# A second Strassen step shared by pairs of text units, in the output projection of a two-attention block

## The chip, the cores and the metric

One core of one Trainium2 chip. The metric is device time in microseconds (us) of one execution of the whole program; lower is better. TensorE is PE in the profile, its weight loads PEld, VectorE is DVE, ScalarE is ACT, GpSimd is POOL, and SyncE is SP.

## What is computed

The input x is 2 batches of 2048 rows of 640 float32, beside a context of 2 x 128 rows of 384, whose last 4 rows are "adapter" tokens. There are 8 heads of 80 columns.

```
query = x @ Wq;  keyt = ctx[:, :124] @ Wk;  valt = ctx[:, :124] @ Wv
hs = mha(query, keyt, valt)                    # text attention, 2048 x 124 scores a head
ca_q1 = einsum(adapter, Wq_ca)[:, indices, :]
ca_hs1 = mha(ca_q1, x, x)                      # adapter attention, x is key and value
ca_hs2 = mha(ca_hs1 @ Wq, adapter @ Wk_ca, adapter @ Wv_ca)
out = (hs + ca_hs2) @ Wout + b_out + x
```

Everything is float32. The place of the change is the product hs @ Wout for the text path.

## The kernel before, in words

**Units.** The 4096 rows of x are 16 *text units* m of 256 rows, each two tiles i of 128 rows. For a unit the kernel computes scores (`sc`), a softmax (`p`, `r`), turns the probabilities with DVE (`eb`), stores them to DRAM (`kept<-eb`) and takes them back turned as `pT`. Then `text_out_fast(m)` does three products `ph` (hidden rows, turned: features on the partitions), copies them on ACT or DVE into a set of buffers `hs` and a fifth chunk of 128 features that lies in a buffer named `wout_sums`, and makes four sums s1 to s4 of blocks of `hs` on DVE or POOL.

**The first Strassen step.** hs of a unit is split in 2 halves of its rows by 2 halves of its first 512 features, Wout in 2 by 2 with halves of 320 columns (`HALF`). With sums t1 to t4 of the weight blocks (`wsum`, in `wout_sums`, too) seven instead of eight block products give the output, and the last 128 features are multiplied plainly (the "fifth"). The products are put into four *chains* `po_m_0` to `po_m_3` of 4, 2, 1 and 1 steps. A chain keeps one PSUM bank of 128 x 320: a step's matmuls add to what is there, then DVE adds the bank into a half row tile of x (tiles `x_more` or `last_rows`), and the next step of the chain waits for that add, since it changes the bank. So the place of the output that a step belongs to gets all that the chain has summed so far. There are 8 such adds in a unit and 128 in all.

**by_columns.** Every block product runs as four matmuls of 128 x 32 weights, on four strips of columns side by side, 4 to a chunk of 128 features. In the order, "32x320 x8" is a product of two chunks. In the trace a float32 matmul has two records, so that product has 16.

**Order.** Nothing is scheduled at run time. `Desk` issues the operations of all coroutines in the order of a table `TURNS` written into the kernel, from the path of a coroutine to a number for each of its operations: the smallest number goes next, and its remainder by 6 names the engine. Each engine then runs its own instructions in that order, waiting on semaphores where its operands are not there. A step, its add and the next step are operations of one coroutine, so the table has to place them one after another, but other work of PE and of DVE stands between them.

**Other rooms.** `kept` stores, one for each half unit, are 32 in all; the exponentials of the adapter path use buffers `e`, `eb`, `rests`, `landing` and `q` that are free once text scores, softmax and stores are done. Rows of x, 8 tiles, are held from their load until the unit's store. For the last unit (15) the output is stored in halves of a row as each is ready; for others POOL first adds the adapter's rows by an indirect DMA (`add_second`).

Helpers collect line numbers. Before, L396 is any matmul, L405 the matmuls of `by_columns`, L427 an operation of DVE, ACT or POOL, L447 a DMA. After, they are L424, L433, L455 and L475.

Of the kernel before, what the change touches and what calls it, by code (L numbers as in the profile page):

```python
# [14 lines left out]
P = 128  # L15
# [50 lines left out]
class Desk:  # L66
# [393 lines left out]
def kernel(  # L460
# [410 lines left out]
    def one(op):  # L871
        yield op
# [199 lines left out]

    def wq_turned():

        yield Do("DVE", lambda: columns(wq_sb, wq4), [("wq", c) for c in range(5)], marks=["wq4"])
        for i in range(NCH):
            if i < 4:
                op = yield Do("NONE", lambda at: wide_rows[at[0]], [], needs=[(first_rows, 1)])
# [1513 lines left out]
```

## Time and profile before

| what | value |
|---|---|
| median of 3 executions | 573.56 us (573.53 to 573.89) |
| the profiled execution | 572.92 us, of which its span 570.9 us |
| PE busy | 563.0 us, 99%, 8069 records |
| PEld busy | 309.6 us, 54% |
| DVE busy | 394.5 us, 69%, 659 records |
| ACT busy | 287.1 us, 50% |
| POOL busy | 160.1 us, 28% |
| matmuls `po` by columns | 2304 records of 128 x 320 |
| granted PE clock | 1.0 |

The span is what the profile's records cover; the time of the profiled execution is 2.02 us above it. Busy shares are means over the span: the first 400 us hold the adapter path, text scores and softmax, the last 160 us mainly `ph`, the output products and the rest of the adapter path.

### The profile page before, as it was taken

The page shows a single profiled execution, that of the slowest core. Times are in us where ns is not written, and L with a number is a line of the kernel's source. Part 1 is how long each engine was busy: PE and PEld are TensorE (multiplying, and loading weights), DVE is VectorE, ACT ScalarE, POOL GpSimd, SP SyncE. Part 2 cuts the span into 40 slices and gives each one's busy share as a digit, 9 for nine tenths or more (in the row PEclk, how much of TensorE's full clock was granted, in tenths as well). Part 3 has the DMA queues.
Part 4 walks back from the last instruction along what each step waited for, and adds up shares of the span by engine and source line. Part 5 has one row for each costly group of instructions (what it writes and reads, how often), then busy time and mean ns, then how long its engine had stood idle before and what let it go on. Part 6 is the DMA issues. An engine that isn't in the chain of part 4 may idle for free.

```text
span 570.9 us, 18875 instructions
## 1 busy us (share of the span) xinstructions
PE 563.0 (99%) x8069; PEld 309.6 (54%) x8069; DVE 394.5 (69%) x659; ACT 287.1 (50%) x806; POOL 160.1 (28%) x213
## 2 busy tenths in 40 slices
PE   8999999999999999999999999999999999999997
PEld 8885335455555455466554554555555554455553
DVE  4366999999998577458999999998332213544443
ACT  2021355645566899899885754534554664100000
POOL 9102041114440731100004350531203053045152
PEclk9999999999999999999999999999999999999999
DMA  8998476965968977446646979987476587788888
GB/s 245 219 239 141 125 160 154 175 179 133 209 214 153 221 177 214 149 123 201 228 153 201 328 187 316 224 241 228 94 248 131 167 185 243 251 217 212 255 182 209
DMA packets 145691, 113.21 MB, mean 198 GB/s; under 512 B 82548, under 2 KB 116980, under 8 KB 145608
## 3 DMA queue, kind: packets, MB, share of 16 engines
q1 hardware_dynamic: 137144, 95.43, 59.9%
q0 software_dynamic: 5632, 10.69, 11.6%
q10 hardware_dynamic: 2832, 5.90, 3.0%
q8 instruction: 63, 1.03, 0.8%
q14 instruction: 20, 0.16, 0.1%
HBM read 71.60 MB, written 40.39 MB: 196 GB/s over the span
## 4 chain that ended last, share of the span: by engine, by line
PE 93%; ACT 3%; DVE 3%; DMA 1%; issue 0%; SPq 0%; ACTq 0%
PE po L405 28%; PE pq L405 24%; PE sc L396 8%; PE acc L396 7%; PE ph L396 7%; PE s L396 7%; PE pq L396 4%; PE pyz L396 2%; ACT ea L427 2%; PE pv L396 1%; DVE mx L427 1%; PE pk L396 1%; DMA xz<-in_x_dram 1%; ACT p L427 1%; PE pt_wq L410 1%; PE pw L396 0%
## 5 line engine op out<-in xcount | busy, mean ns | idle before, releaser
L427 ACT ACTIVATE p<-sc,m 128x124 f32<-128x124 f32 x256 | 90.4, 382 | 43.0 <-DVE m L427 38.0
L427 DVE TENSOR_REDUCE mx<-s 128x4 f32<-128x2048 f32 x48 | 109.0, 2270 | 1.9 <-PE s L396 1.9
L427 ACT ACTIVATE ea<-s 128x2048 f32<-128x2048 f32 x48 | 90.5, 1886 | 30.9 <-PE s L396 30.5
L405 PE MATMUL po<-wout_sums,hs 128*32 128x320 f32 x1024 | 78.4, 434 | 0.1
L405 PE MATMUL po<-wout_sb,hs 128*32 128x320 f32 x928 | 72.3, 433 | 0.0
L427 POOL TENSOR_TENSOR p<-p,r 128x992 f32<-128x992 f32 x17 | 31.4, 1849 | 130.9 <-DVE r L427 130.9
L405 PE MATMUL pq<-xt,wq_sb 128*32 128x256 f32 (+1 forms) x928 | 66.4, 418 | 0.0
L427 DVE TENSOR_TENSOR last_rows<-last_rows,po 128x320 f32<-128x320 f32 x60 | 28.0, 480 | 44.0 <-PE po L405 43.8
L427 ACT ACTIVATION_READ_ACCUMULATOR p<-sc,m 128x1 f32 x256 | 57.2, 223 | 0.0
L427 DVE TENSOR_TENSOR x_more<-x_more,po 128x320 f32<-128x320 f32 x68 | 32.3, 480 | 34.2 <-PE po L405 33.7
L405 PEld LDWEIGHTS po<-wout_sums,hs 128*32 128x32 f32 x1024 | 33.4, 110 | 32.7 <-issue 2.7
L427 DVE TENSOR_REDUCE m<-sc 128x4 f32<-128x496 f32 x64 | 40.7, 661 | 14.1 <-PE sc L396 14.0
L396 PE MATMUL acc<-ea,y_sb 128*32 128x384 f32 (+2 forms) x768 | 50.2, 382 | 0.2 <-ACT ea L427 0.2
L396 PE MATMUL ph<-pT,vpad 128*32 128x256 f32 x768 | 47.7, 381 | 0.0
L405 PEld LDWEIGHTS po<-wout_sb,hs 128*32 128x32 f32 x928 | 30.1, 110 | 28.3 <-issue 1.6
L2351 POOL DMA_INDIRECT x_more<-o,query x17 | 26.6, 1564 | 65.2 <-DVE x_more L427 31.1
L405 PEld LDWEIGHTS pq<-xt,wq_sb 128*32 128x32 f32 x928 | 27.7, 110 | 28.0 <-issue 13.5
L427 ACT COPY hs<-ph 128x512 f32<-128x512 f32 (+1 forms) x25 | 13.4, 552 | 57.7 <-PE ph L396 57.7
L427 DVE STREAM_TRANSPOSE eb<-p 128x1024 f32<-128x1024 f32 x32 | 39.4, 1232 | 1.2 <-POOL p L427 1.1
L396 PEld LDWEIGHTS sc<-kmain,q 64*128 64x128 f32 x512 | 31.8, 187 | 12.6 <-issue 5.8
L427 POOL TENSOR_TENSOR hs<-hs 128x256 f32<-128x256 f32 x31 | 28.9, 1020 | 33.7 <-ACT hs L427 25.4
L396 PE MATMUL sc<-kmain,q 64*128 64x124 f32 x512 | 38.0, 285 | 0.0
(219 smaller groups left out, 834.4 us busy)
## 6 DMA issues: line engine op xcount, KB each, us to landing
kept<-eb SPq DMA_DIRECT2D x32, 512.0 KB, 3.5
pT<-kept SPq DMA_DIRECT2D x16, 1024.0 KB, 8.0
landing<-away SPq DMA_DIRECT2D x15, 512.0 KB, 4.8
xi<-in_x_dram SPq DMA_DIRECT2D x56, 128.0 KB, 4.2
x_more<-in_x_dram SPq DMA_DIRECT2D x17, 320.0 KB, 5.0
last_rows<-in_x_dram SPq DMA_DIRECT2D x15, 320.0 KB, 4.8
y<-yt SPq DMA_DIRECT2D x16, 256.0 KB, 3.9
y_sb<-y SPq DMA_DIRECT2D x32, 128.0 KB, 4.0
```

The source lines that it names most:

```text
L396: self.pin(self.nc.tensor.matmul(out, lhsT, rhs, **kw))
L405: self.pin(self.nc.tensor.matmul(out[j : j + 32], lhsT[:, j : j + 32], rhs, **kw))
L410: self.pin(self.nc.tensor.transpose(out, in_, ident))
L427: self.pin(getattr(engine, what)(*args, **kw))
L2351: desk.pin(nc.gpsimd.indirect_dma_start(out=t, out_offset=None, in_=o2_of[b], in_offset=bass.IndirectOffsetOnAxis(ap=query[:, st : st + 1] ...
```

## The change

**Pairs.** Ten of the sixteen units form five pairs, (6,7), (3,12), (9,14), (10,11) and (8,15), and units take their turns with the output in the order 0, 4, 2, 1, 5, 13, then the pairs, instead of 0 to 15. A paired unit keeps chain 0 (4 steps) and the product s3·t3, whose bank is now added to two places of the output. The other three block products of the first step, a01·w10, s4·w11 and a11·t4, are taken out of the unit. For each of them the two units of a pair are laid one above the other, 256 rows by 256 features by 320 columns, and that is split again in 2 by 2 by 2: `joint` makes seven products of 128 rows, 128 features and 160 columns instead of eight, in four chains `pi_n_p_c` of 4, 2, 1 and 1 steps (n the pair, p = 0, 1, 2 the block product, c the chain), with the fifth chunk's products in the last steps of the chains. Each of their 8 steps is followed by a DVE add of 128 x 160 into a quarter of a row tile: 24 for a pair.

**Inner sums.** `take_inner` waits for all `kept` stores, then takes the freed buffers (`e`, named `p_0` and `p_1` in the order, `eb`, `rests`, `landing`, one `q`) and makes 12 inner sums of the weights, `inner_w`, once. `joint` makes 8 sums of hs blocks for a pair, `inner_x` (4 of 256 columns, 4 of 128), on DVE or POOL.

**Last unit and beginning.** The last unit's one single-step chain left, s3·t3, is computed in two column halves of 160, and its first tile is stored in quarters of a row. In `wq_turned` the copy `wq4` is forked off, and the first transposes of a chunk wait for that chunk of Wq alone.

**TURNS** is replaced as a whole; a line of it:

```diff
-        ".1": [1025], ".2": [44, 59, 60, 84, 96, 108, 114, 120, 126, 132, 150, 174, 198, 210, 234, 1002], ".3":
```

The core of the rest:

```diff
-        yield Do("DVE", lambda: columns(wq_sb, wq4), [("wq", c) for c in range(5)], marks=["wq4"])
+        yield Fork(one(Do("DVE", lambda: columns(wq_sb, wq4), [("wq", c) for c in range(5)], marks=["wq4"])), 2)
...
-                op = yield Do("PE", turn, ["wq4"], needs=[(banks, 1)])
+                op = yield Do("PE", turn, ["wq4" if c0 else ("wq", i)], needs=[(banks, 1)])
...
+        if m in pair_of_unit:
+            chains = (chains[0], (((s3, t3, None), [("hs", m, "s3")], ((1, 1), (1, 0))),))
...
+    PAIRED = ((6, 7), (3, 12), (9, 14), (10, 11), (8, 15))
...
+    def take_inner():
+        yield Do("NONE", lambda: None, ["wsum"] + [("kept", m, k) for m in range(UNITS) for k in range(2)])
+        op = yield Do("NONE", lambda *z: None, [], needs=[(es, 2), (ebs, 1), (rests, 2), (landing, 1), (qslots, 1)])
...
+    def joint(n, pair):
...
+            steps_of = (
+                (([(a[0][0], w[0][0])], [], (0, 0)), ([(s2, t2)], x(1), (1, 0)), ([(s1, t1)], x(0), (0, 1)),
+                 ([fifth(1, 1)], ends_h, (1, 1))),
+                (([(s3, t3)], x(2), (1, 1)), ([(a[1][1], t4), fifth(1, 0)], ends_h, (1, 0))),
+                (([(a[0][1], w[1][0]), fifth(0, 0)], ends_h, (0, 0)),),
+                (([(s4, w[1][1]), fifth(0, 1)], x(3) + ends_h, (0, 1)),),
+            )
+            for c, steps in enumerate(steps_of):
+                yield Fork(inner_chain(n, pair, p, c, steps, (of4 if p == 1 else []) + ends_h + rows_in, rank), rank)
...
+    def inner_chain(n, pair, p, c, steps, ready, rank):
...
+            op = yield Do(
+                "PE", product, after + at + ready, needs=[(banks, 1)] if k == 0 else [], mode=(P, 32), rank=rank
+            )
...
+            def add(r=r, v=v, po=po):
+                t = xr_of[pair[r]][i][0][:, u * HALF + v * HALF // 2 : u * HALF + (v + 1) * HALF // 2]
+                desk.b_tensor_tensor(t, t, po[:, : HALF // 2], ALU.add)
+            op = yield Do(
+                "DVE", add, [op.at], frees=[(banks, s)] if end else [], marks=[("isum", n, p, r, v, c)], rank=1
+            )
+            at = [op.at]
```

**What it moves.** In the whole program the matmul instructions of the output products by columns go from 1152 of 320 columns to 784 of 320 and 676 of 160. PSUM adds on DVE go from 128 of 128x320 to 106, with 124 of 128x160 beside them.

On PE at the very end, where unit 15's chains close, before (`po_15_0` is the chain of four steps; the number behind a name is its buffer's):

```order
L405 MATMUL po_15_0_7039<-wout_sums_4129,hs_0_4130 32x320 x8
L405 MATMUL po_15_3_7094<-wout_sb_100,hs_0_4130 32x320 x12
L405 MATMUL po_15_1_7110<-wout_sums_4129,hs_0_4130 32x320 x8
L405 MATMUL po_15_0_7039<-wout_sums_4129,hs_0_4130 32x320 x8
L405 MATMUL po_15_1_7110<-wout_sums_4129,hs_0_4130 32x320 x8
L405 MATMUL po_15_1_7110<-wout_sb_100,hs_0_4130 32x320 x4
L405 MATMUL po_15_0_7039<-wout_sb_100,hs_0_4130 32x320 x4
```

The same place after (`pi_4_...` are the products of the fifth pair, units 8 and 15; rows with `wout_sums` on the right of the comma are the fifth chunk):

```order
L433 MATMUL po_15_0_None_7573<-wout_sb_100,hs_1_4231 32x320 x8
L433 MATMUL pi_4_1_0_7453<-wout_sb_100,wout_sums_4140 32x160 x4
L433 MATMUL po_15_1_0_7591<-wout_sums_4140,hs_1_4231 32x160 x8
L433 MATMUL po_15_0_None_7573<-wout_sums_4140,hs_1_4231 32x320 x8
L433 MATMUL pi_4_0_0_7431<-wout_sb_100,wout_sums_4140 32x160 x4
L433 MATMUL pi_4_1_1_7562<-p_1_844,hs_1_4231 32x160 x4
L433 MATMUL pi_4_1_1_7562<-wout_sb_100,wout_sums_4140 32x160 x4
L433 MATMUL po_15_0_None_7573<-wout_sums_4140,hs_1_4231 32x320 x8
L433 MATMUL pi_4_2_1_7425<-inner_w_5507,hs_1_4231 32x160 x4
L433 MATMUL pi_4_2_1_7425<-wout_sb_100,wout_sums_4140 32x160 x4
L433 MATMUL po_15_0_None_7573<-wout_sb_100,wout_sums_4140 32x320 x4
L433 MATMUL po_15_1_1_7654<-wout_sums_4140,hs_1_4231 32x160 x8
```

Between two steps of `po_15_0` there were three products of 320 or one; now there are pieces of 160, and before its last step two pieces of four matmuls. The first half of s3·t3 has moved ahead, the second closes the program.

On DVE, where the inner sums of the weights are made, before (`last_rows` and `x_more` are row tiles, `eb` turned probabilities):

```order
L427 TENSOR_TENSOR p_0_830<-p_0_830,r_1_15_5049 128x32x31
L427 STREAM_TRANSPOSE eb_15_1_5489<-p_0_830 128x1024
L427 TENSOR_TENSOR hs_0_4130<-hs_0_4130 128x256
L427 TENSOR_TENSOR last_rows_4240<-last_rows_4240,po_6_2_5452 128x320
L427 COPY hs_2_5064<-ph_7_2_5514 128x512
```

And after; the last `eb` row is now that of unit 12:

```order
L455 STREAM_TRANSPOSE eb_12_1_5429<-p_1_844 128x1024
L455 COPY wout_sums_4140<-ph_6_4_5431 128x256
L455 COPY hs_2_5067<-ph_7_0_5453 128x512
L455 TENSOR_TENSOR x_more_3084<-x_more_3084,po_5_1_None_5465 128x320
L455 TENSOR_TENSOR last_rows_4230<-last_rows_4230,po_13_1_None_5311 128x320
L455 TENSOR_TENSOR inner_w_5507<-wout_sums_4140 128x160 x2
L455 COPY hs_2_5067<-ph_7_2_5477 128x512
L455 TENSOR_TENSOR p_0_843<-wout_sb_100 128x160
L455 TENSOR_TENSOR p_1_844<-wout_sb_100,p_1_844 128x160
```

Four rows stand between the last turn of probabilities and the first write into the buffer `inner_w`, which is the room of an `eb` before it.

More of the change, by code (lines that the diff above doesn't have):

```diff
@@ L2247, in probabilities @@
         op = yield Do(
-            "NONE", lambda z: wide("pT", z[0], f"pT_{m}"), needs=[(pTs, 1)], marks=[("back", m)],
+            "NONE", lambda z: wide("pT", z[0], f"pT_{m}"), needs=[(pTs, 1)], marks=[("back", m), ("taken", m)],
         )
@@ L2457, in product @@
                         by_columns(
-                            to[:, :HALF], l, r, start=(k == 0 and c == 0), stop=(c == len(pairs) - 1),
+                            to[:, cols], l, r[:, cols], start=(k == 0 and c == 0), stop=(c == len(pairs) - 1),
                             skip_group_check=True,
@@ L2489, in text_out_fast @@
             if m < UNITS - 1:
-                yield Fork(stored(m, i, reads[i, 0] + reads[i, 1]), 1)
+                yield Fork(stored(m, i, reads[i, 0, 0] + reads[i, 1, 0]), 1)
             else:
                 for u in range(2):
-                    yield Fork(stored_half(m, i, u, reads[i, u]), 1)
+                    for v in range(2) if i == 0 else (None,):
+                        yield Fork(stored_half(m, i, u, v, reads[i, u, 0] + reads[i, u, 1] if v is None else reads[i, u, v]), 1)
         for n, steps in enumerate(chains):
-            yield Fork(chain(n, steps), 30 + m)
+            for part in (0, 1) if n in apart else (None,):
+                yield Fork(chain(n, steps, part), 30 + turn_of[m])
@@ L2497, with inner_of_w @@
     fast_of = {}
-    def stored_half(m, i, u, ends):
+    PAIRED = ((6, 7), (3, 12), (9, 14), (10, 11), (8, 15))
+    pair_of_unit = {m: (n, r) for n, pair in enumerate(PAIRED) for r, m in enumerate(pair)}
+    inner_w, inner_x, xjs = [], [], Room(0)
+    OF_HS = {0: (0, 0), 1: (0, 1), 2: (1, 0)}
+    def inner_of_w(p):
+        if p == 2:
+            w = wsum[3]
+        else:
+            w = wout_sb[:, 2:4, p * HALF : (p + 1) * HALF]
+        return [[w[:, k, n * HALF // 2 : (n + 1) * HALF // 2] for n in range(2)] for k in range(2)]
@@ new lines, in take_inner, with less @@
+    def take_inner():
+        yield Do("NONE", lambda: None, ["wsum"] + [("kept", m, k) for m in range(UNITS) for k in range(2)])
+        op = yield Do("NONE", lambda *z: None, [], needs=[(es, 2), (ebs, 1), (rests, 2), (landing, 1), (qslots, 1)])
+        at_q = op.slots[4][0]
+        t = late["pool"].tile([P, 4 * HEADS * R], F32, tag="eb", name="inner_w")
+        flat = [e.rearrange("p h n -> p (h n)") for e in late["e"]] + [t]
+        inner_w.extend(t[:, : 2 * HALF].rearrange("p (s n) -> p s n", s=4) for t in flat)
+        for p in range(3):
+            w, to = inner_of_w(p), inner_w[p]
+            for i, x, y, after in (
+                (0, w[0][1], w[0][0], []), (2, w[1][1], w[0][1], []), (1, w[1][1], to[:, 0], [("iw", p, 0)]),
+                (3, w[1][0], to[:, 1], [("iw", p, 1)]),
+            ):
+                def less(to=to, i=i, x=x, y=y):
+                    (desk.g_tensor_tensor if desk.engine == "POOL" else desk.v_tensor_tensor)(to[:, i], x, y, ALU.subtract)
+                yield Fork(one(Do(("DVE", "POOL"), less, after, rank=0, marks=[("iw", p, i)])), 0)
+        yield Do("NONE", lambda: None, [("iw", p, i) for p in range(3) for i in range(4)], marks=["inner w"])
+        t = q_slot(at_q, "inner_x0")
+        a = late["pool"].tile([P, 2 * 4 * P], F32, tag="rests", name="inner_x1")
+        b = late["pool"].tile([P, 4, 2 * P], F32, tag="landing", name="inner_x2")
+        for ends, middle in ((t.rearrange("p s n -> p (s n)")[:, : 8 * P], t[:, 2:3].rearrange("p s n -> p (s n)")),
+                             (a, b.rearrange("p s n -> p (s n)")[:, : 4 * P])):
+            inner_x.append((
+                ends.rearrange("p (s q n) -> p s q n", s=4, q=2), middle.rearrange("p (s n) -> p s n", s=4),
+            ))
+            xjs.at.append(desk.now)
@@ new lines, in joint, with sums, fifth @@
+    def joint(n, pair):
+        rank = 30 + turn_of[pair[0]]
+        of2 = [("hsT", m, 2) for m in pair]
+        of4 = [("hs", m, "s4") for m in pair]
+        op = yield Do("NONE", lambda z: z[0], of2 + ["inner w"], needs=[(xjs, 1)])
+        at_x = op.value
+        ends, middle = inner_x[at_x]
+        hs = [fast_of[m][0][0] for m in pair]
+        last = [[fast_of[m][0][1][:, i * P : (i + 1) * P] for i in range(2)] for m in pair]
+        five = [wout_sb[:, 4, u * HALF : (u + 1) * HALF] for u in range(2)]
+        outer = [[hs[r][:, 2 + k].rearrange("p (q t) -> p q t", q=2) for k in range(2)] for r in range(2)]
+        inner = [[hs[r][:, 7].rearrange("p (c t) -> p c t", c=2)[:, k] for k in range(2)] for r in range(2)]
+        for name, a, to, after in (("e", outer, ends, of2), ("m", inner, middle, of4)):
+            for i, x, y, op_of, more in (
+                (2, a[0][0], a[1][0], ALU.subtract, []), (0, a[1][0], a[1][1], ALU.add, []),
+                (1, to[:, 0], a[0][0], ALU.subtract, [("ix", n, name, 0)]),
+                (3, a[0][1], to[:, 1], ALU.subtract, [("ix", n, name, 1)]),
+            ):
+                def sums(to=to, i=i, x=x, y=y, op_of=op_of):
+                    (desk.g_tensor_tensor if desk.engine == "POOL" else desk.v_tensor_tensor)(to[:, i], x, y, op_of)
+                yield Fork(one(Do(("DVE", "POOL"), sums, after + more, marks=[("ix", n, name, i)], rank=1)), 1)
+        ends_h = [("hsT", m, 4) for m in pair]
+        rows_in = [("xr", m) for m in pair]
+        for p in range(3):
+            name, a, s = ("m", inner, middle) if p == 1 else (
+                "e", [[outer[r][k][:, p // 2] for k in range(2)] for r in range(2)], ends[:, :, p // 2]
+            )
+            w, t = inner_of_w(p), inner_w[p]
+            i_, u_ = OF_HS[p]
+            def fifth(r, v, i_=i_, u_=u_):
+                return last[r][i_], five[u_][:, v * HALF // 2 : (v + 1) * HALF // 2]
+            s1, s2, s3, s4 = [s[:, i] for i in range(4)]
+            t1, t2, t3, t4 = [t[:, i] for i in range(4)]
+            x = lambda i, name=name: [("ix", n, name, i)]
+            steps_of = (
[7 more added lines that the diff above has]
+                yield Fork(inner_chain(n, pair, p, c, steps, (of4 if p == 1 else []) + ends_h + rows_in, rank), rank)
+        yield Do(
+            "NONE", lambda: None, [("inner", n, p, c) for p in range(3) for c in range(4)], frees=[(xjs, at_x)],
+            marks=[("joined", n)],
+        )
@@ new lines, in inner_chain, with product @@
+    def inner_chain(n, pair, p, c, steps, ready, rank):
+        po, s, at = None, None, []
+        for k, (pairs, after, (r, v)) in enumerate(steps):
+            def product(s=None, k=k, pairs=pairs):
+                to = bank(s[0], f"pi_{n}_{p}_{c}") if s else po
+                for j, (l, w) in enumerate(pairs):
+                    by_columns(
+                        to[:, : HALF // 2], l, w, start=(k == 0 and j == 0), stop=(j == len(pairs) - 1),
+                        skip_group_check=True,
+                    )
+                return to
+            op = yield Do(
+                "PE", product, after + at + ready, needs=[(banks, 1)] if k == 0 else [], mode=(P, 32), rank=rank
+            )
+            if k == 0:
+                po, s = op.value, op.slots[0][0]
+            end = k == len(steps) - 1
+            if end:
+                desk.event(("inner", n, p, c)).t = op.at.t
+            i, u = OF_HS[p]
+            def add(r=r, v=v, po=po):
+                t = xr_of[pair[r]][i][0][:, u * HALF + v * HALF // 2 : u * HALF + (v + 1) * HALF // 2]
+                desk.b_tensor_tensor(t, t, po[:, : HALF // 2], ALU.add)
+            op = yield Do(
+                "DVE", add, [op.at], frees=[(banks, s)] if end else [], marks=[("isum", n, p, r, v, c)], rank=1
+            )
+            at = [op.at]
@@ L2501, in stored_half, with inner_sums @@
+    def inner_sums(m, i, u):
+        n, r = pair_of_unit[m]
+        for p in range(3):
+            if OF_HS[p] == (i, u):
+                at = {(0, 0): (0, 2), (1, 0): (0, 1), (0, 1): (0, 3), (1, 1): (0, 1)}
+                return [("isum", n, p, r, v, c) for v in range(2) for c in at[r, v]]
+        return []
+    def stored_half(m, i, u, v, ends):
         b, st = tiles(m)[i]
         cols = slice(u * HALF, (u + 1) * HALF)
+        if v is not None:
+            cols = slice((2 * u + v) * HALF // 2, (2 * u + v + 1) * HALF // 2)
@@ L2505, in stored_half @@
         to = out[b, st * P : (st + 1) * P, cols]
[L2506 removed]
+        yield Do(("SP", "ACT"), lambda: dma(to, t[:, cols], 0.43 if v is None else 0.25, 0.45, 2.2))
     def stored(m, k, both):
```

60 lines of the change are left out of this document (38 added, 22 removed), and 439 rows, old and new, of the table TURNS.

## The prediction

> **What bounds the kernel now.** I read the page first: busy time, the slices, the chain that ended last.
>
> ```profile
> span 570.9 us, 18875 instructions
> PE 563.0 (99%) x8069; PEld 309.6 (54%) x8069; DVE 394.5 (69%) x659; ACT 287.1 (50%) x806; POOL 160.1 (28%) x213
> PE   8999999999999999999999999999999999999997
> DVE  4366999999998577458999999998332213544443
> PEclk9999999999999999999999999999999999999999
> PE 93%; ACT 3%; DVE 3%; DMA 1%; issue 0%; SPq 0%; ACTq 0%
> ```
>
> PE is busy in every slice at full granted clock, and 93% of the chain is PE. So matmul time taken away shortens the kernel, unless PE has to wait. DVE is full in slices 5 to 12 and 19 to 28 and then drops to 2 to 5 tenths. Then the windows of the last 160 us, where the products of the change lie (start and end, length, busy time and count of PE, PEld, DVE, ACT, POOL, clock, DMA):
>
> ```profile
> 400.00:440.00 40.00, 40.00 (x652) 20.36 (x648) 14.03 (x27) 21.93 (x15) 9.48 (x7) 1.00 0.59 155
> 440.00:480.00 40.00, 40.00 (x646) 20.00 (x639) 10.21 (x22) 23.64 (x18) 9.23 (x10) 1.00 0.76 212
> 480.00:520.00 40.00, 40.00 (x623) 20.01 (x619) 18.54 (x46) 6.31 (x10) 13.60 (x11) 1.00 0.82 217
> 520.00:560.00 40.00, 40.00 (x620) 22.32 (x612) 17.88 (x42) 1.54 (x3) 18.62 (x14) 1.00 0.84 206
> ```
>
> PE never waits here, and DVE has 60.7 us of work in 160 (14.03 + 10.21 + 18.54 + 17.88). Last, PE's list of waits: for whom, how long in all, how often, the longest.
>
> ```profile
> PE s L396 <- DVE mx L427: 1.1, 2, 0.7
> PE pt_x L410 <- DVE first_rows L427: 0.4, 1, 0.4
> ```
>
> There is little to win from waits, so the sum is about streamed columns, and about the waits that the change can bring.
>
> **The stream.** The products by columns, and stretches of the timeline of PE in which such matmuls run without a stop (start, length, count):
>
> ```profile
> L405 PE MATMUL po<-wout_sums,hs 128*32 128x320 f32 x1024 | 78.4, 434 | 0.1
> L405 PE MATMUL po<-wout_sb,hs 128*32 128x320 f32 x928 | 72.3, 433 | 0.0
> L405 PE MATMUL po<-wout_sb,wout_sums 128*32 128x320 f32 x352 | 31.1, 432 | 0.0
> ...
> 388.00 2.34 PE L405 MATMUL po<-wout_sb,hs 128*32 128x320 f32 x32
> 390.16 1.26 PE L405 MATMUL po<-wout_sums,hs 128*32 128x320 f32 x16
> 391.35 0.44 PE L410 MATMUL pm<-ident,mt 128*128 128x128 f32 x2
> ...
> 52.89 1.00 PE L396 MATMUL pvca<-w_vca,caT 128*32 128x160 f32 x24
> 53.70 1.90 PE L405 MATMUL pq<-xt,wq_sb 128*32 128x512 f32 x16
> ```
>
> The 2304 records are the 1152 matmuls. Four run side by side, so one's 433 ns isn't its price: that is the distance of the starts, (390.16 - 388.00)/32 = 67.5 ns a record. The trace has records of 160 columns in the same shape of tile, too: (53.70 - 52.89)/24 = 33.75 ns, half. The change takes away 368 matmuls of 320, 736 records, 49.7 us, and adds 676 of 160, 1352 records, 45.6 us. That is **-4.05 us**. The starts are rounded to 0.01 us, which is 0.6 us over the 1352 records and 0.2 over the others.
>
> What speaks against so clean a half are the weight loads, one to each record whatever its width:
>
> ```profile
> 52.89 0.67 PEld L396 LDWEIGHTS pvca<-w_vca,caT 128*32 128x32 f32 x20 [0.30 <-issue]
> ```
>
> Twenty take 0.67 us, 33.5 ns each, just under the 33.75 of the matmuls beside them. They are hidden with nothing to spare. On this the Trainium skill, "TensorE: Matmul & The Clock Gate", section "Back-to-back issue gap", says that in a stream of load and matmul pairs both set the spacing, about 81 ns at 128 columns where the formula for one alone gives 56. If 160-column records paid that ratio, 45.6 us would be about 66 (an estimate from that page) and the kernel some 20 us slower. The row above disagrees: 33.75 ns at 160 columns with a load to each.
>
> A change of tile shape costs 1.19 us (391.35 - 390.16) for 16 records of 1.08, 0.11 us; along PE's order there are three more of them: **+0.3**.
>
> **New waits in the chains.** A step's successor waits for a DVE add. From the end of the program and a place where adds follow each other:
>
> ```profile
> 562.19 3.44 PE L405 MATMUL po<-wout_sums,hs 128*32 128x320 f32 x48
> 563.53 0.49 DVE L427 TENSOR_TENSOR x_more<-x_more,po 128x320 f32<-128x320 f32 x1 [2.21 <-PE po L405]
> 565.42 1.29 PE L405 MATMUL po<-wout_sb,hs 128*32 128x320 f32 x16
> 566.23 1.03 DVE L427 TENSOR_TENSOR x_more<-x_more,po 128x320 f32<-128x320 f32 x2 [0.61 <-PE po L405]
> ...
> 402.92 0.47 DVE L427 TENSOR_TENSOR last_rows<-last_rows,po 128x320 f32<-128x320 f32 x1
> 403.31 0.48 DVE L427 TENSOR_TENSOR x_more<-x_more,po 128x320 f32<-128x320 f32 x1
> ...
> L427 DVE TENSOR_TENSOR x_more<-x_more,po 128x320 f32<-128x320 f32 x68 | 32.3, 480 | 34.2 <-PE po L405 33.7
> L427 DVE TENSOR_TENSOR wq_sums<-pq,wq_sums 128x256 fp32r<-128x256 f32 x7 | 2.9, 411 | 0.4 <-ACT wq_sums L427 0.4
> ```
>
> The first 16 records of the stretch from 562.19 end at 563.27, the add starts at 563.53: 0.26 us to the start, 0.48 for it, so a successor needs 0.75 us of other work between. Going from 256 to 320 columns adds 69 ns, so 160 are about 480 - 2.5 x 69 = 0.31 us, and 0.57 of other work do. I laid the rows between each two steps of a chain against this, at the prices above. Before, 64 successors have one gap under 0.9 us and none too short. After, 114 successors have 16 under 0.9, two of them 0.54: one of 160 columns, short by 0.03, and the last step of `po_15_0` with two pieces of four matmuls of 160 ahead of it, short by 0.21. DVE runs in order, and an add that has another right in front comes 0.39 us later (403.31 - 402.92). Going along DVE's order with each row at its price, seven of the steps come 0.10 to 0.35 us late, 1.5 us in all: **+1.5**. The ends are 0.24 (no add ever behind another) and 7.7 (each of 16 late by a whole 0.48 add).
>
> **DVE and POOL.** DVE loses 22 adds of 0.48 us and gains 124 of 0.31, 29 sums, and five copies that ACT had:
>
> ```profile
> L427 DVE TENSOR_TENSOR hs<-hs 128x256 f32<-128x256 f32 x33 | 16.2, 496 | 5.5 <-POOL hs L427 5.3
> L427 DVE COPY hs<-ph 128x512 f32<-128x512 f32 x11 | 7.5, 683 | 15.4 <-PE ph L396 10.5 <-issue 4.9
> L427 DVE TENSOR_TENSOR p<-p,r 128x992 f32<-128x992 f32 x6 | 7.1, 1188 | 0.1
> L427 POOL TENSOR_TENSOR hs<-hs 128x256 f32<-128x256 f32 x31 | 28.9, 1020 | 33.7 <-ACT hs L427 25.4 <-DVE hs L427 7.8
> ```
>
> That is 124 x 0.31 - 22 x 0.48 + 11 (11 sums of 0.496, 18 narrower ones at about 0.3) + 5 x 0.68, some 42 us more: 103 of 160, 64%. It fits, so it costs nothing by itself; its cover is the third of DVE that stays idle. POOL gets 16 sums of x of at most 1.02 us and 7 of weights, at most 23 us beside 50.9, and fits too. In the last 14 us 28 narrow and 7 wide adds are 12 us, DVE at 84%: there the cover is thin, and five of the 16 short gaps lie there. On this the Trainium skill, "TensorEngine Tiling (Array Packing)", section "PSUM Bottleneck", warns that tiling speeds TensorE, not the emptying of PSUM, and advises both ScalarE and VectorE for it. The windows above agree so far that 320-wide adds did not bind; no row shows it for 160, and by that rule rival A would come.
>
> **Places that are only moved.** DVE loses two products `p<-p,r` of 1.19 us that stood ahead of one of its `mx` stalls of PE: I take 0.3 of the 1.1 us off (bounds 0 and 1.1): **-0.3**. In the start the first transposes no longer wait for `wq4`; the 0.4 us wait for `first_rows` may go or come again elsewhere: **0**, within 0.6 either way. At the end the last product's two adds of 160 take 0.62 us where the last two of 320 took 1.03, but the product before them stands later; the store behind the last add is as before: **0**, within 0.4.
>
> **Sum.** -4.05 + 0.3 + 1.5 - 0.3 = -2.55 us on the profiled execution's 572.92, so 570.37; the median of the runs is 0.64 above that execution, so **571.0**.
>
> **Rivals.**
>
> **A, slower: DVE's queue in front of the short gaps.** If in front of every short gap there is one foreign add (0.39), the 23 gaps up to 1.1 us fall short by 4.3 us in all; with 1.3 of them by 6.7, with two by 13. At 1.3 the sum is -4.05 + 0.3 + 6.7 = +2.95: **576.5**. It decides from about 0.95 foreign adds per short gap, where the 4.05 are gone. For it: 84% DVE at the end, and copies of 0.68 among the adds. Against it: 64% over the whole stretch, and a PE that is late lets DVE catch up, so that shortfalls don't all add.
>
> **B, about the same: DVE stands at the inner weights.** Their first write goes to the room of an `eb`, and has to wait until its store has landed.
>
> ```profile
> 437.80 1.24 DVE L427 STREAM_TRANSPOSE eb<-p 128x1024 f32<-128x1024 f32 x1
> ...
> 444.98 0.52 SPq L447 DMA_DIRECT2D kept<-eb  x1
> ...
> kept<-eb SPq DMA_DIRECT2D x32, 512.0 KB, 3.5
> ```
>
> Here SP, behind its loads, issued the last store 5.9 us after the transposition's end (444.98 - 439.04), and landing takes 3.5: 9.4 us. In the new order PE has about 11.3 us of rows from that transposition to the first step that needs a result from behind the write, and DVE about 3.9 us of work in between. So with SP as late as here PE stands 9.4 + 3.9 - 11.3 = 2.0 us: -0.55, **573.0**. If SP issues at once, it costs nothing; the loads of rows ahead of it in SP's order leave both open.
>
> **C, the whole gain:** only the 0.24 us of short gaps, both `mx` stalls and 0.6 us of the start gone: -4.05 + 0.3 + 0.24 - 1.1 - 0.6 = -5.2, **568.3**.
>
> **D, the narrow records pay for their loads.** 338 sets of four (676 x 2 / 4) with one load more exposed, 0.13 us (4 x 33.5 ns), are 44 us: **616**. The 24 records above exclude it nearly.
>
> **Chances.** The forecast 0.57; C 0.13, B 0.12, A 0.16, D 0.02. 0.2% of the time, 1.15 us, is about what a measurement of this kernel can tell from no change. Faster by more than that: the forecast, C, less a few hundredths of the forecast's upper end: 0.68. Same: B and that end: 0.14. Slower: A and D, 0.18. The range goes from 568.6, most of C, to 574.8, where A has one foreign add in front of each short gap (+0.55, 574.1) and a little beyond: it leaves out A's upper part, D and C's lower.
>
> **What would show it.** Right: PE's records of 160 columns start 33.7 ns apart; PE's busy time in the last 160 us falls by about 4 us; in the list of waits `po` and `pi` stand with about 1.5 us on DVE's adds, mostly at `po_15_0` and in the last 40 us; DVE at 60 to 65% in the windows. Wrong: records of 160 further apart than 34 ns (D); several us of waits of `pi` and `po` on `x_more` and `last_rows` (A); one wait of PE near 420 us behind `inner_w`, with DVE idle on a DMA (B); or a change of several us in the first 400 us, which this sum leaves out.

## The result, and the profile after

The changed kernel took 580.48 us (580.20 to 582.72, 4 runs) against 573.65 (573.53 to 573.89): 6.8 us slower by medians, and the ratio over the runs is 1.0128 with a 95% interval of 1.0106 to 1.0150. Of all executions below two are left out, both of the experiment "Both edits", at 585 us and a granted clock of 0.99. The forecast was 571.0, with 574.8 as its upper end. The profiled execution took 580.75 us, 7.8 more than the one of before, its span 579.0, 8.1 more. Busy times, slices and the engines' shares of the chain that ended last:

```profile
span 579.0 us, 20311 instructions
PE 564.4 (97%) x8685; PEld 327.8 (57%) x8685; DVE 426.8 (74%) x793; ACT 284.0 (49%) x807; POOL 179.5 (31%) x239
DVE  4265999989998576455999999996564345657584
PE 75%; DVE 12%; ACT 6%; issue 3%; DMA 1%; SPq 1%; POOL 1%; DVEq 0%; ACTq 0%; POOLq 0%
```

PE went from 99% of the span to 97%, and its share of the last chain from 93% to 75%; DVE's went from 3% to 12%. The same four windows as before, then PE's list of waits:

```profile
400.00:440.00 40.00, 40.00 (x710) 21.82 (x704) 23.53 (x49) 20.61 (x14) 16.63 (x20) 1.00 0.71 189
440.00:480.00 40.00, 39.95 (x735) 22.43 (x727) 17.14 (x45) 21.60 (x14) 14.48 (x15) 1.00 0.64 181
480.00:520.00 40.00, 38.12 (x763) 24.34 (x760) 24.64 (x74) 7.03 (x9) 12.20 (x11) 1.00 0.70 191
520.00:560.00 40.00, 39.37 (x796) 26.63 (x792) 27.55 (x79) 2.50 (x5) 22.06 (x19) 1.00 0.88 227
```

```profile
PE s L424 <- DVE mx L455: 2.4, 3, 1.2
PE pi L433 <- DVE inner_x L455: 0.8, 2, 0.6
PE pi L433 <- DVE x_more L455: 0.7, 2, 0.5
PE po L424 <- DVE o L455: 0.3, 1, 0.3
PE ph L424 <- DVE last_rows L455: 0.3, 1, 0.3
PE po_None L433 <- DVE x_more L455: 0.2, 1, 0.2
```

DVE is at 92.9 us of the 160, 58%, less than forecast, and yet PE now loses 2.5 us in the last two windows, where it lost nothing. Not all of these waits are of a successor in a chain: `inner_x` is a product that waits for a sum of hs blocks, `o` a copy of the adapter path, and in the row of `ph` a bank comes free too late.

**Where the 8.1 us of span came from.** Three places can be told apart by when the same instruction starts in both traces. First, the products `pyz` of the adapter path, which both kernels have at the same places of PE's order (before, then after):

```profile
166.52 1.53 PE L396 MATMUL pyz<-xt,wyz 64*32 64x512 f32 x24
```

```profile
169.85 1.95 PE L424 MATMUL pyz<-xt,wyz 64*32 64x512 f32 x32
```

By 167 us, long before the first pair, the changed kernel is 3.3 us late. The lag came in steps: 1.0 us by 50 us, 2.2 at 125, 3.3 at 167, and it stays at about 3. One step in the timeline of DVE and PE:

```profile
120.93 0.67 DVE L455 TENSOR_REDUCE m<-sc 128x4 f32<-128x496 f32 x1
123.10 1.31 DVE L455 STREAM_TRANSPOSE xt<-xi 128x512 f32<-128x512 f32 x2 [1.50 <-DMA rows_w<-w_sb]
124.33 2.26 DVE L455 TENSOR_REDUCE mx<-s 128x4 f32<-128x2048 f32 x1
126.64 0.50 PE L424 MATMUL s<-zop,cop 32*128 32x512 f32 x4 [1.17 <-DVE mx L455]
```

DVE, busy for 37.7 us of the 40 from 120 us on, stands for 1.50 us until a DMA has landed, the maximum `mx` behind it is late, and PE waits 1.17 us for the bank that `mx` reads. The row names `rows_w`, a store, but only as the latest DMA of one of several semaphores that the transposition waits for; by the times of all of them it was most likely a load of x, issued at 119.01 us and landed at 122.98. Second, the pairs: the last matmul record of PE starts at 572.28 us, in the kernel before at 566.27. So the lag grew from 3.0 us at 238 us to 6.0 although PE streams fewer columns. Third, the end: from that start to the end of the span it is 6.7 us, before 4.6. The three make up the 8.1: 3.0, 3.0 and 2.1.

```profile
566.70 1.55 POOL L2380 DMA_INDIRECT x_more<-o,query  x1 [2.47 <-DVE last_rows L455]
571.26 2.35 ACTq L475 DMA_DIRECT2D out_dram<-last_rows  x2
572.69 0.55 DVE L455 TENSOR_TENSOR last_rows<-last_rows,po 128x160 f32<-128x160 f32 x2
574.16 0.34 ACTq L475 DMA_DIRECT2D out_dram<-x_more  x1
```

The last sum ends at 573.2, but the last store issued, at 574.16, is a whole row tile of unit 8, unit 15's partner. Its sums close late, at 566.4, then POOL adds the adapter's rows by the indirect DMA of 566.70. That one lands at 574.14 by its semaphore, and the store follows at once; ACT's queue had been free from 573.61.

### The profile page after: what moved, and what is told of

It is laid out like the page before. It is cut to its first block, busy times and chain, and to the rows that moved or that the text cites. A ratio compares the mean times of both kernels' runs of the same rounds, so it can differ in the third digit from the quotient of the medians.

```text
span 579.0 us, 20311 instructions
## 1 busy us (share of the span) xinstructions
PE 564.4 (97%) x8685; PEld 327.8 (57%) x8685; DVE 426.8 (74%) x793; ACT 284.0 (49%) x807; POOL 179.5 (31%) x239
## 4 chain that ended last, share of the span: by engine, by line
PE 75%; DVE 12%; ACT 6%; issue 3%; DMA 1%; SPq 1%; POOL 1%; DVEq 0%; ACTq 0%; POOLq 0%
PE pq L433 18%; PE po_None L433 15%; PE pi L433 8%; PE acc L424 6%; PE s L424 6%; PE ph L424 6%; PE sc L424 4%; DVE mx L455 4%; PE pq L424 3%; ACT p L455 3%; ACT ea L455 2%; PE pyz L424 2%; DVE x_more L455 1%; DVE eb L455 1%; PE pv L424 1%
## 5 line engine op out<-in xcount | busy, mean ns | idle before, releaser
L455 POOL TENSOR_TENSOR p<-p,r 128x992 f32<-128x992 f32 x18 | 33.4, 1854 | 153.8 <-DVE r L455 153.8
L433 PE MATMUL po_None<-wout_sums,hs 128*32 128x320 f32 x848 | 66.0, 434 | 0.1
L433 PE MATMUL po_None<-wout_sb,hs 128*32 128x320 f32 x568 | 44.4, 434 | 0.2 <-DVE x_more L455 0.2
L455 DVE TENSOR_TENSOR x_more<-x_more,po_None 128x320 f32<-128x320 f32 x60 | 28.2, 477 | 19.8 <-PE po_None L433 19.6
L455 ACT COPY hs<-ph 128x512 f32<-128x512 f32 (+1 forms) x21 | 11.2, 537 | 61.8 <-PE ph L424 30.0
L433 PEld LDWEIGHTS po_None<-wout_sums,hs 128*32 128x32 f32 x848 | 26.3, 109 | 23.8 <-issue 1.4
L455 POOL TENSOR_TENSOR hs<-hs 128x256 f32<-128x256 f32 x32 | 27.6, 910 | 32.7 <-DVE hs L455 32.4
L2380 POOL DMA_INDIRECT last_rows<-o,query x15 | 23.3, 1552 | 42.6 <-DVE last_rows L455 31.9
L424 PEld LDWEIGHTS ph<-pT,vpad 128*32 128x32 f32 x768 | 24.5, 110 | 18.4 <-issue 1.4
```

What stands on the lines that cost most here:

```text
L424: self.pin(self.nc.tensor.matmul(out, lhsT, rhs, **kw))
L433: self.pin(self.nc.tensor.matmul(out[j : j + 32], lhsT[:, j : j + 32], rhs, **kw))
L455: self.pin(getattr(engine, what)(*args, **kw))
L2380: desk.pin(nc.gpsimd.indirect_dma_start(out=t, out_offset=None, in_=o2_of[b], in_offset=bass.IndirectOffsetOnAxis(ap=query[:, st : st + 1] ...
```

## The experiments

Twelve kernels. Where the table is rearranged, it was sorted anew from both kernels' orders, and all numbers change; the diff then shows one entry as an example.

**The first 300 us in the order of before** (all operations but those of the pairs and row tiles). The changed table gives 39 of these 1304 operations to another engine than the table of before, and they go back, too:

```diff
-        ".1": [683],
+        ".1": [659],
```

> The changed kernel with the first 300 us of its table put back into the order of the kernel before (1304 operations; the pairs and all that follows as changed). Theory 1, the reordered first part costs about 3 us of its own: weight products pyz of the adapter path start 1.0 us later than before at 50 us, 2.2 at 125, 3.3 at 167 and still 3.0 at 240 in the changed kernel's trace, so this kernel should come out at 580.5 - 3.0 = 577.5 (577.0 to 578.2), with lag near 0 at 240 us. Rival, the first part is not to blame, and what is gained there is waited for again at the pairs: 580.0 to 580.8.

Measured 576.84 us (576.02 to 577.12): 3.6 us of the 6.8 are gone. In its trace the product that lay at 166.52 before starts at 166.96.

```profile
166.96 1.95 PE L909 MATMUL pyz<-xt,wyz 64*32 64x512 f32 x32
```

Theory 1 holds, the rival falls: what is lost there isn't gained again at the pairs.

**The first 60 us only.** The same, with 228 operations.

> As above, but only the first 60 us (228 operations) in the order of the kernel before. Theory 1a, the start itself costs the 1.0 us of lag seen at 50 to 100 us and the rest comes from DVE waiting for loads of x near 122 us: 579.5. Theory 1b, the whole 3 us follow from the start, since DVE is full from 80 to 160 us and can't make up what it loses: 577.5. Rival, the start is not to blame: 580.5.

579.24 us (578.75 to 579.73), 1.2 less: theory 1a by its time. But its trace has another course: the wait of `xt` near 122 us is 0.3 us instead of 1.5, and the lag is 0 at 49 us, 1.4 at 78, after a wait of 1.4 us for `mx`, and 2.0 at 167. So that one load isn't what the rest hangs on.

**The first 200 us.** The same, with 863 operations.

> The changed kernel with the first 200 us of its table (863 operations, all engines and queues) in the order of before. The lag of the products pyz was 3.3 us at 167 us and did not grow after, so this should give nearly all that the first 300 us gave: 577.2 (576.5 to 577.8). Rival, the rest of the gain lies between 200 and 300 us: 578.5.

577.15 us (576.67 to 577.78), 3.3 less, as much as the lag at 167 us. 25 of the 863 operations change their engine with it.

**The same first part without pairs:** the kernel before with the changed order of the first 300 us, the forked copy and its waits.

```diff
-        yield Do("DVE", lambda: columns(wq_sb, wq4), [("wq", c) for c in range(5)], marks=["wq4"])
+        yield Fork(one(Do("DVE", lambda: columns(wq_sb, wq4), [("wq", c) for c in range(5)], marks=["wq4"])), 2)
...
-                op = yield Do("PE", turn, ["wq4"], needs=[(banks, 1)])
+                op = yield Do("PE", turn, ["wq4" if c0 else ("wq", i)], needs=[(banks, 1)])
```

> The kernel before with the first 300 us of the changed kernel's order (and the forked copy of Wq and its waits), no pairs. Theory 1, the reordered first part costs its own time wherever it stands: 573.7 + 3.0 to 3.6 = 577. Rival, it costs only in front of the pairs, since before has room to make it up later: 573.7 to 574.3.

577.0 us, as theory 1 says, but with a spread from 574.14 to 578.78, where the kernel before stays within 573.3 to 574.8 in all but one of 21 runs beside it. In the profiled one (575.8 us) a wait for a DMA is the longest, one that the kernel before doesn't have:

```profile
PE ph L808 <- DMA pT<-kept: 1.7, 1, 1.7
```

So the first part costs by itself, 3.4 us in the median, and part of its cost hangs on when loads land: in this trace the lag is 1.5 us at 167 us, not 3.3, and the wait above adds to it later.

**Only the queue of loads of the first 200 us in the order of before:** SyncE's entries, all else as changed.

> The changed kernel with only SyncE's queue (loads and stores) of the first 200 us in the order of before, all other engines in the changed order. Theory 1c, what the first part loses is that DVE waits for loads that come later in SyncE's new order (1.5 us at 122 us for a load of x, then 1.35 us of PE for the maximum behind it): 577.5 to 578.5. Theory 1d, it is the new order of work on PE and DVE, which the loads of before can't mend: 580.0 to 581.

587.16 us (583.88 to 590.81), worse than either order. Both theories fall in this form: this queue of loads, made for one order of work, doesn't fit the other. PE's waits name new places:

```profile
PE ph L909 <- DMA pT<-kept: 4.2, 1, 4.2
PE pq L918 <- DVE q L940: 2.4, 2, 2.1
PE pt_wq L923 <- DVE ctxT L940: 2.0, 1, 2.0
```

The lag is 7.2 us at 238 us, against 3.0 in the changed kernel. So this run doesn't tell whether the changed first part loses by its loads, by the order of its work or by the operations that it gives to other engines.

**Unit 8 without the adapter's rows:**

```diff
-        op = yield Do("POOL", lambda: add_second(t, b, st), [*both, ("o2", b), "query"])
+        op = yield Do("POOL", lambda: add_second(t, b, st) if m != 8 else None, [*both, ("o2", b), "query"])
```

> The changed kernel without the POOL indirect DMA that adds the adapter's rows to the two row tiles of unit 8 (this part of its output is left out), so that these tiles are stored as soon as their sums are there. Theory 2, the end of the program is unit 8's: its last sum is at 566.4, the indirect DMA is issued at 566.7, the store at 574.2 and the span ends at 579.0, where unit 15's own last sum at 573.2 would end it 3.6 us later, at 576.9. So 2.1 us less: 578.4. Rival, the end is unit 15's last stores, which only queue behind one another: 580.0 to 580.8.

579.57 us, but from 577.85 to 582.65; the ratios' intervals (1.0067 to 1.0148 here) overlap with the changed kernel's, so the 0.9 us are not shown by the times. In the timeline of its ACT queue the store of unit 8's tile is still the last, right behind the two others:

```profile
571.55 2.35 ACTq L475 DMA_DIRECT2D out_dram<-last_rows  x2
574.00 0.41 ACTq L475 DMA_DIRECT2D out_dram<-x_more  x1
```

The span ends 4.4 us after the last sum at 573.5, in the changed kernel 5.7. But in the kernel with the early order, which keeps the indirect DMA, it ends 4.1 us after it. So in the changed kernel's trace the store waits for the indirect DMA, but no more than 0.5 us (574.16 against 573.61), and the runs don't show that it costs anything steadily.

**Narrow products alone.** The kernel before, each product of 320 as two of 160; its output is another, so it serves for the time alone.

```diff
-                        by_columns(
-                            to[:, :HALF], l, r, start=(k == 0 and c == 0), stop=(c == len(pairs) - 1),
+                        for v in range(2):
+                            cols = slice(v * HALF // 2, (v + 1) * HALF // 2)
+                            by_columns(
+                                to[:, cols], l, r[:, cols], start=(k == 0 and c == 0), stop=(c == len(pairs) - 1),
```

> The kernel before with each product of 320 columns made as two of 160 into the two halves of its bank; sums on DVE as before. It measures what 160 columns cost: sets of four records take 0.136 us in the changed kernel's trace, sets of 320 0.269, so 576 sets become 1152 and PE has 576 x 0.003 = 1.7 us more: 575.3. By the prediction's 33.75 against 67.5 ns a record it is 573.6. If a set of narrow records exposes one weight load of 0.13 us, it is some 75 us or more above.

591.27 us (588.43 to 596.58), 17.6 us slower, and none of the three numbers. PE's list of waits has a new first row, "issue", for which the list names no cause:

```profile
PE po L405 <- issue: 8.9, 10, 2.0
```

One of these places in the timeline of PE:

```profile
403.75 0.45 PE L405 MATMUL po<-wout_sb,hs 128*32 128x160 f32 x8
406.19 0.48 PE L405 MATMUL po<-wout_sb,hs 128*32 128x160 f32 x8 [1.99 <-issue]
```

And PE's queue of instructions on the page (packets, MB, share), before and in this kernel:

```profile
q8 instruction: 63, 1.03, 0.8%
```

```profile
q8 instruction: 81, 1.33, 0.9%
```

Ten such stops of 0.4 to 2.2 us lie inside products, where no semaphore is waited for. From one to the next there are 127, 254, 510, 636, 639, 764, 892 or 1150 matmul records, always close to a multiple of 127.5. With a load to each record that is 255 instructions. A packet of the queue is 16.4 KB (1.33 MB in 81), and the 18 packets more than before go with 4608 more records and loads, 256 to a packet. The trace has the time of each packet, too: all ten stops end 1.3 to 1.5 us after one has come in. So PE stands for instructions at the ends of blocks where narrow products follow one another for long. By the distances of the starts the ten stops take 10.7 of the 18.9 us by which this span is longer (589.8 against 570.9). Inside products, between the stops, sets of four records of 160 columns mostly keep to 0.136 us, which is the 1.7 us of the expectation; the remaining 6.5 us lie in part behind the longest stop, where the granted clock is 0.50 for 3.4 us, and are otherwise open. In the changed kernel no product stops inside for more than 0.25 us: its narrow products stand between wide ones.

**Thin sums at the pairs.** On the kernel with the early order of before (576.84 us); the rest of these products' columns is left out.

```diff
-                desk.b_tensor_tensor(t, t, po[:, : HALF // 2], ALU.add)
+                desk.b_tensor_tensor(t[:, :8], t[:, :8], po[:, :8], ALU.add)
```

> The kernel with the early order of before (576.8), and in it the 120 sums of the pairs from PSUM 8 columns wide instead of 160 (the other columns of these products are left out of the output). Theory 3, the pairs wait on DVE: PE's waits after 400 us are about 5 us longer there than in the kernel before, and DVE loses 120 x 0.2 = 24 us of work, so the waits shrink by 2 to 3 us: 574.3. Rival, what is waited for is the order (a sum behind others that are not ready, the time from PE to DVE and back), not DVE's work: 576.3 or more.

574.83 us (573.75 to 578.25, 10 runs), 2.0 less, as theory 3 says. Nine of the ten lie under the lowest run without this edit (576.02), though the two ratios' intervals, 1.0011 to 1.0040 and 1.0032 to 1.0066, overlap a little.

**No inner sums of hs blocks at the pairs.** On the same kernel.

```diff
-        for name, a, to, after in (("e", outer, ends, of2), ("m", inner, middle, of4)):
+            ("e", [[z[:, :, :4] for z in r] for r in outer], ends[:, :, :, :4], of2),
+            ("m", [[z[:, :8] for z in r] for r in inner], middle[:, :, :8], of4),
...
-            s1, s2, s3, s4 = [s[:, i] for i in range(4)]
+            s1, s2, s3, s4 = a[1][0], a[0][0], a[1][1], a[0][1]
```

> The kernel with the early order of before (576.8); the sums of hs blocks for the second Strassen step are made 8 columns wide, and its products read blocks of hs in their place (this part of the output is not computed), so no product waits for them. Theory 3a, the inner sums, made one after another on POOL and DVE, are what PE waits for at the pairs (0.7 us in the list of waits of that kernel, and adds that stand behind them): 575.3. Rival, the sums of PSUM alone: 576.5.

576.35 us (575.88 to 577.82), 0.5 less: nearer to the rival, and not clear of the noise (the ratios' intervals, 1.0037 to 1.0072 and 1.0032 to 1.0066, are nearly the same). In its trace no product waits for `inner_x` any more, but PE waits for a load, which it doesn't in the kernel without this edit:

```profile
PE ph L909 <- DMA pT<-kept: 1.2, 1, 1.2
```

So the inner sums may cost more than the 0.5 us.

**Both edits.**

> The two edits together. What is left of the change is its saved stream on PE with hardly any new work for DVE. If the stream saves 3.5 us (sets of four records of 160 columns 0.136 us, of 320 0.269, in the traces) and the end costs about 0.5, this is 573.7 - 3.5 + 0.5 = 570.7, up to 572 with waits that stay. Rival, narrow records cost more than half of wide ones by seams and a slow supply of instructions, so the stream saves nothing: 573.7 or more.

573.80 us (median of eight, 573.21 to 575.81): ratio to before 1.0006, interval 0.9991 to 1.0022. So with most of its new work for DVE gone, the change gives nothing, where I had expected 3 us. The windows of 480 to 560 us of the kernel with the early order, and of this one (columns as above):

```profile
480.00:560.00 80.00, 77.91 (x1563) 52.54 (x1567) 53.23 (x159) 7.65 (x13) 34.59 (x30) 1.00 0.81 207
```

```profile
480.00:560.00 80.00, 79.05 (x1645) 59.30 (x1640) 40.70 (x167) 7.09 (x13) 32.46 (x31) 1.00 0.83 214
```

PE's idle time falls from 2.1 to 0.95 us. What is left of it is mainly 0.5 us for the copy of `o` and 0.3 for a sum of a chain; and the span ends 5.3 us after the start of the last matmul record, 0.7 more than before.

**Eighteen copies given to ACT.** On the kernel with the early order; the number's remainder by 6 names the engine.

```diff
-        ".62.3.1": [6146],
+        ".62.3.1": [6145],
```

> The kernel with the early order of before (576.8), and the 18 copies of PSUM into hs and its fifth chunk that DVE makes after 395 us given to ACT, which has 54 us of work in the last 160. DVE loses 18 copies of 0.4 to 0.7 us, 11 us in all. Theory 3, DVE's work is what PE waits for at the pairs; 24 us less of it in the sums gave 2.0 us, so 11 us should give 0.5 to 1.0: 576.0. Rival, copies stand where DVE has time: 576.8.

577.49 us (577.03 to 577.95), 0.6 more, not less, though the 0.6 are within the noise (interval of the ratio 1.0051 to 1.0084). Taking the copies off DVE, 11.9 us of its work between 400 and 560 us (93.8 to 81.9), doesn't help; making the sums thin, 13.9 us (to 79.9), did. This points to the time of the sums that stand in a chain or right ahead of one, rather than to DVE's load. It doesn't prove it: PE now waits 0.4 us for a copy on ACT, so a small gain may be hidden.

**And the inner sums given to POOL.** As above, with entries such as

```diff
-        ".79.1": [6476],
+        ".79.1": [6471],
```

> As above, and the 24 inner sums of hs blocks that DVE makes given to POOL, too (about 1.0 us each on POOL for 256 columns, 0.5 on DVE). Theory 3 says DVE loses another 10 us, 575.5; but the sums follow one another, and POOL's longer time and its indirect DMAs between them make products wait. I expect that the second wins: 577 to 579.

584.44 us (583.41 to 585.69), far more than expected. PE's list of waits names it:

```profile
PE pi L918 <- POOL inner_x L940: 5.7, 4, 2.1
```

Where they stand, the inner sums cost little that the times show; on POOL, a slower engine for them that works on indirect DMAs between them, they are waited for at once.

## Why the prediction was wrong, step by step

**The stream was right in its price, but little of it came through.** In the changed kernel's timeline narrow products run at

```profile
508.81 0.57 PE L433 MATMUL pi<-wout_sb,hs 128*32 128x160 f32 x8
509.08 0.57 PE L433 MATMUL pi<-wout_sb,wout_sums 128*32 128x160 f32 x8
510.24 0.48 PE L433 MATMUL pi<-p,inner_x 128*32 128x160 f32 x8 [0.59 <-DVE inner_x L455]
```

0.27 us for 8 records, 33.75 ns each. Over all sets of four the medians are 0.136 us for 160 columns and 0.269 for 320, which makes the term -3.5 in place of -4.05. These are prices inside products. From the start of each record of the output products to the next start on PE 159.0 us pass in all before, 160.6 after, and 157.9 with both edits: what the narrow products save is lost between the products, and even with both edits only 1.2 us of it come through. Rival D is excluded here, though the run with nothing but halves shows that narrow products can be far dearer, by another mechanism than D's. The rule of the Trainium skill, "TensorE: Matmul & The Clock Gate", section "Back-to-back issue gap", isn't borne out by either trace: the spacing inside products stays at about 34 ns.

**"Places that are only moved", the start: 0, within 0.6. This step failed: half of the whole loss was put at nothing.** It measured 3.3 us in the first 200 us, 3.6 in the first 300 (the runs with that much of the order put back). I had taken the waits there from the trace of before, whose windows show what was overlooked:

```profile
80.00:120.00 40.00, 40.00 (x571) 19.80 (x566) 39.74 (x55) 21.95 (x80) 5.61 (x4) 1.00 0.78 171
```

DVE is full there, 39.74 of 40 us, so what DVE loses there has no cover, and PE can lose it too, as in the row of 126.64 us. How much it would lose could not be read from the trace of before. The prediction did name several us in the first 400 as a sign that it is wrong.

**New waits in the chains: +1.5. This step failed, too: the term was mis-sized.** PE's lag behind the kernel before grows from 3.0 us at 238 us to 6.0 at the last record, while the stream is 3.5 us shorter by its prices: 6.5 us of waits and of time between products, where the sum had 1.5 and the 0.3 for shapes. Only 2.6 us of them stand in PE's list as idle time. Thin sums bring 2.0 us, both edits 3.0. Beside the successors that I had counted, PE waits for things that I had costed at nothing since DVE and POOL had room. The row of 510.24 above is one, a product that waits 0.59 us for an inner sum on DVE:

```profile
508.81 0.32 DVE L455 TENSOR_TENSOR last_rows<-last_rows,pi 128x160 f32<-128x160 f32 x1 [2.38 <-PE pi L433]
509.17 0.49 DVE L455 TENSOR_TENSOR last_rows<-last_rows,po_None 128x320 f32<-128x320 f32 x1
509.57 0.52 DVE L455 TENSOR_TENSOR inner_x<-hs,hs 128x128 f32<-128x128 f32 x1
```

The sum has no wait of its own in the trace, but DVE makes it behind two adds, and the first of these stood 2.38 us for its product. Others are a bank behind four narrow sums and the copy of `o`. The last step of `po_15_0`, said to come 0.21 late, came 0.25 us late by the starts of the records. Rival A, foreign adds in front on DVE, gave 576.5 with the first part and the end at nothing; the kernel with the first 300 us put back took 576.84. So for the pairs alone A's size was nearer than the forecast's, and thin sums give back 2.0 of the 3.2 us that are left there against before (573.67); how much of the rest is A's isn't shown. The rule of the Trainium skill, "TensorEngine Tiling (Array Packing)", section "PSUM Bottleneck", that the emptying of PSUM may become the bottleneck, agrees with these 2.0 us. DVE's load, 58%, doesn't show it; the copies given to ACT point to the time of single sums.

**The end: 0, within 0.4.** From the start of the last matmul record to the end of the span it is 6.7 us in the profiled execution, 2.1 more than before, and 5.1 to 6.1 in the ten other traces with pairs, 0.5 to 1.5 more. I looked at the last product's sums and took unit 15's store as the end; the row tile of unit 8, which the pairing makes late, was overlooked. What makes the end longer in one trace than in another is open.

**Rivals B and C.** In DVE's list of waits the inner weights have a row, and PE waits for nothing there: B did not come.

```profile
DVE inner_w L455 <- DMA kept<-eb: 0.3, 1, 0.3
```

C, the whole gain, isn't reached even with most of the new work for DVE gone (573.80).

**The sum.** Against before in medians: 6.8 us, of which 3.6 are the first part, 3.0 the sums of the pairs (576.84 to 573.80), and 0.2 all the rest: in that last trace the output products gain 1.2 us, and PE's other products (0.8) and the end (0.7) lose more. Open is whether the first part loses by its queue of loads, by its order of work or by the operations given to other engines; the run meant to part the first two fitted neither. No version here beats the kernel before.

## What to carry to other kernels

Before calling a moved stretch free, look for the engine that is full there: what it loses has no cover. A step that saves matmul columns by making more and smaller partial sums can pay for it between the products, even where the engine that makes the sums has room: count the gap of each successor, what stands ahead of each sum in its engine's order, and the banks. And compare the time from start to start, for idle time alone shows only a part of it (2.6 of 6.5 us here). And when work of two tiles is joined, ask which tile now ends last, and what still has to be done to it.

## What the runs showed of the hardware

PE can outrun its instructions. Where 160-column products (33.75 ns a matmul record with its load) follow one another for long, it stops for 0.4 to 2.2 us at multiples of 127.5 matmul records, ten times in 230 us, each time until 1.3 to 1.5 us after a packet of instructions has come in; the time spreads from 588 to 597 us. The Trainium skill, "Runtime: NRT & Kernel Launch", section "Instruction fetch mechanics", has blocks of 16 KiB or 256 instructions, which agrees with the 16.4 KB of a packet and the 255 instructions between stops; that crossing a block costs mostly nothing, as it says, holds for the kernel before (no stop inside a product above 0.15 us) and not here. That a busy DMA is what makes the block late is likely, but no run varied it: the share is 0.80 in the 2 us ahead of the stop at 404, and 0.86 or more in the 2 us ahead of each of the ten packets, against a mean of 0.75 from 310 to 585 us.

```profile
402.00:404.00 2.00, 2.00 (x68) 1.81 (x56) 1.30 (x1) 1.55 (x1) 1.02 (x1) 1.00 0.80 310
```

Behind the stop at 404 the granted clock is 0.50 from 407.4 us for 3.4 us, and sets of four records of 160 columns start 0.27 us apart there instead of 0.136. The run with SyncE's queue shows 0.50, too, from 537.7 us for 6.8 us, beginning in PE's wait of 4.2 us, which ends at 539.2. Other stops of 1.5 to 2.1 us in these two traces have no such dip behind them, so no rule follows.

In the changed kernel two sums of 128 columns on POOL took different times: 1.05 us at 508.36, while the indirect DMA of 507.38 was on POOL, too, and 0.46 at 509.49. Spans on POOL are rough in the profile, and no run parted the two.
